# The router's comparisons behind the decays of level 2: one step moved in a hand-ordered recurrent-mixer kernel

## The chip, the cores and the metric

The kernel runs on one core of a Trainium2 chip. The metric is the time of one execution on the device, in microseconds (us). TensorE (PE), VectorE (DVE), ScalarE (ACT) and GpSimd (POOL) each work through their own queue in order, and wait for one another through semaphores; SyncE (SP) issues the transfers.

## The reference

The input is x, of 2 sequences with 2048 tokens of 256 channels, all in float32. After a layer norm, two branches read it, and the result is x + s * silu(f).

```
xn  = layernorm(x)
# s: the time mixing
dx  = previous token of xn - xn
mix = tanh((xn + dx * x_miu) @ x_A)            # six groups of 32
xd  = xn + dx * (lambdas + mix @ x_B)          # r, w, k, v, a, g
r, v, k, w, a, g = projections of the six xd   # k is normalised to length 1
S   = S * decay + (S a) b^T + v k^T ; y = S r  # per token, 4 heads of 64 x 64
s   = (groupnorm(y) + bonus(r, k, v)) * g @ oW.T
# f: eight experts, two per token
scores = softmax(xn @ gate_w.T + gate_b) ; top 2 -> which experts, and the sum of their scores
f   = sum over the chosen e of gate * (relu(xn @ wi.T + bi + lora_e(xn)) @ wo.T + bo)
```

The top 2 are found by rank: expert e's rank is the number of experts with a larger logit, plus those with an equal logit and a smaller number.

## The kernel before

The tokens are taken in 16 blocks of 256 rows (128 tokens of each of the two sequences). The recurrence of a block is not stepped token by token. In chunks of 64 tokens, the kernel builds the matrix of products between "queries" (AR, which holds a and r) and "keys" (BK, which holds b and k) by levels of run length 1, 2, 4, 8, 16 and 32, inverts it level by level beside that, and then carries the state ST over the chunks.

A block passes through six generators: `norm` (layer norm, transposes), `front` (logits, router, the mix), `mixes` (xd and the projections), `levels` (products and inverse), `chunks` (state, output) and `experts`. Time is counted in turns of 12 units. In one turn the level steps of block n-1 run beside `front` and `mixes` of block n, `chunks` of block n-2 and a share of `experts`. Each generator yields the time at which its next step is due, and the queue at the end of the kernel always runs the step with the smallest time. That fixes the order in which instructions are written, and each engine executes its own in that order. The due times are the numbers in the table `AT`, lines 96 to 107.

The names that the text uses:

- The router, in `front`. L357 (POOL) takes all differences of the logits into eq. The step "gt" follows: L359 (DVE) turns them into gt (greater), L360 (DVE) into eq (equal), L361 (POOL) masks eq and L362 (POOL) adds it to gt. The step "rank" sums gt (L365, DVE) and makes the one-hot oh (L368, DVE, twice).
- The decays, in `decay_on(h)`. After the products of level h are taken, AR is scaled (L587, DVE), BK is scaled (L590, POOL), and the product of the decays over the doubled runs is formed (bp, L592, POOL). For level 2 both are due at 1.94. The products of level 4 (lev, L552, PE) read AR and BK; the inverse step x (L637, PE) follows, is taken into X (L641, DVE), and lev is taken into D (L565, DVE), which m1p (L630, PE) reads.
- Around them: ST (L859, DVE, four per chunk, from the products uv, L846 and L854); miu (L409, PE), which is turned into xd by L415 (DVE, two per group) and L417 (POOL, one per group); the output product op (L909, PE) and the gate after it (L913, DVE); bonb (L746 and L747, POOL); the experts' lop (L951, PE), hs (L955 on DVE, L958 on ACT), hT (L959, POOL), fop (L974, PE) and gate (L976, DVE).

Most products of TensorE go to one ring of four PSUM buffers (`psf`, L63): a product takes the buffer of the fourth one before it, and waits for whoever empties that.

The masks' construction at the start (`constants`) has a step that is due at the time of "gt" too, plus 0.02.

Of the kernel before, what the change touches and what calls it, by code (L numbers as in the profile page):

```python
# [34 lines left out]
def timemix_gated_by_lora_experts(ctx: ExitStack, tc: tile.TileContext, a: dict, out: bass.AP):  # L35
# [50 lines left out]
    def load_x(i):  # L86
# [8 lines left out]

    AT = {
        "stats": 5.73, "root_x": 10.18, "inv_x": 10.27, "xn": 10.83, "xTp": 11.66, "dx": 11.66, "xm": 11.84,
        "lgp": -0.16, "mixp": 0.51, "top": 0.56, "gt": 1.93, "rank": 2.69, "ex": 3.27, "vsum": 4.02, "rp": 4.72,
        "wkp": 5.28, "vp": 6.47, "kp": 7.83, "ssp": 8.61, "dec": 9.04, "ggp": 9.37, "root_k": 9.8, "kn": 10.55,
        "av": 11.71, "rk": 12.04, "bop": 12.53, "eye": -0.33, "query1": 0.39, "key1": 0.54, "query2": 1.94,  # L100
        "key2": 1.94, "query4": 3.29, "key4": 3.49, "query8": 5.43, "key8": 5.46, "query16": 7.8, "key16": 7.86,
# [975 lines left out]
```

## Time and profile before

| | us |
|---|---|
| median of 3 runs | 1079.38 |
| lowest and highest | 1077.13 and 1079.39 |
| profiled execution, its own time | 1079.38 |
| span of its instructions | 1077.6 |
| TensorE busy | 1032.4 |
| VectorE busy | 684.7 |
| GpSimd busy | 666.9 |
| ScalarE busy | 574.8 |

The mean granted clock of TensorE is 0.988 of full speed. A line of the groups or of the timeline names line, engine, operation, and output<-inputs; a timeline line begins with start and length in us, counted from the span's start, and ends in brackets with the idle time of the engine before it and what ended it. The chain of waits is followed back from the last instruction, at each step to what released it. Moments such as 314.85 are on the scale of that span.

### The profile page before, as it was taken

The numbers are of one execution on the slowest core, as the hardware profiler recorded it, in microseconds if no ns is written. First come the engines' busy times: TensorE is split into PE (matmuls) and PEld (weight loads), VectorE is DVE, ScalarE is ACT, GpSimd is POOL, SyncE is SP. The second block draws the span as 40 slices with busy tenths as digits, with TensorE's granted clock in tenths as the row PEclk, the third lists the DMA queues.
The fourth block names the chain that finished last, engine by engine and source line by source line (L and its number), as shares of the span: only waits on it lengthen the run. The fifth ranks groups of instructions, "written<-read, shape, count | busy, mean of one in ns | idle before, by whom it ended". The sixth has DMA issues, their size and how long they took to land.

```text
span 1077.6 us, 51168 instructions
## 1 busy us (share of the span) xinstructions
PE 1032.4 (96%) x23136; PEld 809.9 (75%) x23136; DVE 684.7 (64%) x1613; ACT 574.8 (53%) x1372; POOL 666.9 (62%) x853
## 2 busy tenths in 40 slices
PE   6989999999999998999999999999999999999997
PEld 4667877877778776787777877777777778787775
DVE  5364666767676664756757586665767666666645
ACT  2534647374664736546464655546464554736362
POOL 6473766767485764838657584756757385675541
PEclk9989999999999999999999999999999999999998
DMA  7100000000000000000000000000000000000000
GB/s 217 43 2 2 3 3 4 23 3 23 3 3 23 3 23 2 17 9 4 23 3 23 3 23 3 3 23 4 23 3 13 3 4 13 3 13 3 14 3 21
DMA packets 16153, 17.05 MB, mean 16 GB/s; under 512 B 3328, under 2 KB 15552, under 8 KB 15936
## 3 DMA queue, kind: packets, MB, share of 16 engines
q1 hardware_dynamic: 15776, 13.65, 4.9%
q8 instruction: 182, 2.98, 1.1%
q14 instruction: 35, 0.29, 0.1%
q10 hardware_dynamic: 160, 0.13, 0.0%
HBM read 9.53 MB, written 4.19 MB: 13 GB/s over the span
## 4 chain that ended last, share of the span: by engine, by line
PE 84%; DVE 5%; ACT 3%; issue 1%; POOL 1%; DVEq 0%; POOLq 0%; ACTq 0%
PE fop L974 10%; PE lop L951 10%; PE basep L946 9%; PE lev L552 8%; PE m1p L630 4%; PE m1p L624 3%; PE miu L409 3%; PE rp L426 3%; PE vp L464 3%; PE kp L473 3%; PE x L637 3%; PE op L909 2%; PE mixp L337 2%; PE uv L846 2%; PE sa L816 2%; PE uv L854 1%
## 5 line engine op out<-in xcount | busy, mean ns | idle before, releaser
L959 POOL TENSOR_TENSOR hT<-hs 128x256 f32<-128x256 f32 x128 | 94.3, 737 | 185.8 <-ACT hs L958 185.5
L958 ACT ACTIVATE hs<-hs 128x512 f32<-128x512 f32 x128 | 80.4, 629 | 121.7 <-DVE hs L955 108.3
L951 PE MATMUL lop<-lat,w_lBT 128*128 128x512 f32 x256 | 136.4, 615 | 5.5 <-ACT lat L938 5.2
L955 DVE TENSOR_TENSOR hs<-lop,base 128x512 f32<-128x512 f32 x128 | 87.4, 683 | 83.5 <-PE lop L951 62.8
L946 PE MATMUL basep<-xT,w_wiT 128*128 128x256 f32 x512 | 137.2, 391 | 0.3
L417 POOL TENSOR_TENSOR xd<-xd,xT 128x512 f32<-128x512 f32 x96 | 119.5, 1274 | 13.0 <-DVE xd L415 12.9
L974 PE MATMUL fop<-w_woT,hT 128*128 128x256 f32 x512 | 125.8, 390 | 0.8 <-POOL hT L959 0.8
L946 PEld LDWEIGHTS basep<-xT,w_wiT 128*128 128x128 f32 x512 | 92.1, 191 | 39.4 <-issue 21.7
L565 DVE COPY_PREDICATED D<-mask,lev 128x512 f32<-128x512 uint8 x160 | 106.3, 716 | 16.1 <-PE lev L552 15.9
L552 PE MATMUL lev<-AR,BK 64*64 64x64 f32 x6144 | 110.3, 220 | 3.0 <-POOL BK L590 1.9
L552 PEld LDWEIGHTS lev<-AR,BK 64*64 64x64 f32 x6144 | 99.8, 134 | 16.1 <-issue 8.9
L974 PEld LDWEIGHTS fop<-w_woT,hT 128*128 128x128 f32 x512 | 94.7, 192 | 18.2 <-issue 3.5
L590 POOL TENSOR_TENSOR BK<-BK,bp 128x512 f32<-128x512 f32 x80 | 91.4, 1143 | 15.3 <-PE lev L552 15.3
L415 DVE SCALAR_TENSOR_TENSOR xd<-miu,cvec,dx 128x256 f32<-128x256 f32 x192 | 78.1, 477 | 30.5 <-PE miu L409 30.2
L948 ACT ACTIVATE base<-basep,biT 128x256 f32<-128x256 f32 x128 | 61.0, 476 | 13.2 <-PE basep L946 12.9
L630 PEld LDWEIGHTS m1p<-X,D 64*64 64x64 f32 x2560 | 47.2, 137 | 23.8 <-issue 15.6
L863 ACT COPY Y<-uv 64x128 f32<-64x128 f32 x128 | 33.3, 260 | 52.8 <-DVE ST L859 24.9
L587 DVE TENSOR_TENSOR AR<-AR,bp 128x512 f32<-128x512 f32 x80 | 58.5, 731 | 0.0
L630 PE MATMUL m1p<-X,D 64*64 64x32 f32 x2560 | 54.9, 224 | 3.6 <-DVE D L565 3.5
L641 DVE COPY_PREDICATED X<-maskT,x 128x256 f32<-128x256 uint8 x64 | 32.6, 509 | 38.5 <-PE x L637 38.5
L951 PEld LDWEIGHTS lop<-lat,w_lBT 128*128 128x128 f32 x256 | 43.3, 189 | 15.0 <-ACT lat L938 7.6
L485 POOL TENSOR_TENSOR ksq<-ksq 128x256 f32<-128x256 f32 x16 | 11.6, 727 | 64.7 <-ACT ksq L484 64.7
(218 smaller groups left out, 2369.8 us busy)
## 6 DMA issues: line engine op xcount, KB each, us to landing
x<-in_x SPq DMA_DIRECT2D x32, 128.0 KB, 2.8
out<-x SPq DMA_DIRECT2D x30, 128.0 KB, 2.4
w_wiT<-in_wiT SPq DMA_DIRECT2D x1, 1024.0 KB, 9.3
w_woT<-in_woT SPq DMA_DIRECT2D x1, 1024.0 KB, 7.9
w_lBT<-in_lBT SPq DMA_DIRECT2D x1, 512.0 KB, 6.3
w_rWT<-in_rWT SPq DMA_DIRECT2D x1, 256.0 KB, 5.0
w_vWT<-in_vWT SPq DMA_DIRECT2D x1, 256.0 KB, 8.6
w_kWT<-in_kWT SPq DMA_DIRECT2D x1, 256.0 KB, 3.2
```

Of the source, the lines that this page charges most:

```text
L415: nc.vector.scalar_tensor_tensor(xd[:, c, :], p[:, c, :], cv("lam", c, g), dx[:, c, :], ALU.add, ALU.mult)
L417: nc.gpsimd.tensor_add(xd, xd, xT)
L552: matmul(levp[par][half(b), (k * 2 + pair) * 2 + key], BK[rows, key, c0 : c0 + L], query_runs(AR[rows, c0 : c0 + L, :], h), start=True, st ...
L565: nc.vector.copy_predicated(query_runs(D[:, par, :, 0:L, :], h), mask_of(mask, li, 2 * h, 4 * NK), levp[par])
L590: nc.gpsimd.tensor_mul(ka, ka, decay(1, h).unsqueeze(1).broadcast_to([P, 2, np_, h]))
L630: matmul(m1[half(b ^ k), m], D[half(b), e % 2, (k * 2 + e // 2) * 2, 0:L, 0], runs(X[half(b), m, :], h, 0), start=True, stop=True)
L946: matmul(basep, wiT[:, c, fc], xT[:, c, :], start=(c == 0), stop=(c == 1))
L951: matmul(lop, lBT[:, 0, fc], lat, start=True, stop=True)
L955: nc.vector.tensor_tensor(hs, lop, bs.unsqueeze(1).broadcast_to([P, 2, SUP]), ALU.add)
L958: nc.scalar.activation(hs, hs, AF.Relu)
L959: nc.gpsimd.tensor_add(hT[:, f, :], hs[:, 0, :], hs[:, 1, :])
L974: matmul(fop, hT[:, f, k * P : (k + 1) * P], woT[:, f, :], start=(f == 0), stop=(f == DFF // P - 1))
```

## The change

One number of the table of due times changes. The step "gt" was due at 1.93, just ahead of the decays of level 2 (1.94); it is now due at 2.05, just behind them.

```diff
-        "lgp": -0.16, "mixp": 0.51, "top": 0.56, "gt": 1.93, "rank": 2.69, "ex": 3.27, "vsum": 4.02, "rp": 4.72,
+        "lgp": -0.16, "mixp": 0.51, "top": 0.56, "gt": 2.05, "rank": 2.69, "ex": 3.27, "vsum": 4.02, "rp": 4.72,
```

In the order of the engines' instructions this does the following, in each of the 15 turns that have both steps, and nothing else:

```
VectorE before:  L359 gt, L360 eq, L587 AR
VectorE after:   L587 AR, L359 gt, L360 eq
GpSimd before:   L361 eq, L362 gt, L590 BK, L592 bp
GpSimd after:    L590 BK, L592 bp, L361 eq, L362 gt
```

The orders of TensorE, ScalarE and SyncE are the same in both kernels.

## The prediction

> **What bounds the kernel now.** I read the page first, then the chain of waits in order of time, then the timelines of VectorE and GpSimd around the moved step, and last the busy time of TensorE by stretches. Two lines of the page's first part and its chain by engine:
>
> ```profile
> span 1077.6 us, 51168 instructions
> PE 1032.4 (96%) x23136; PEld 809.9 (75%) x23136; DVE 684.7 (64%) x1613; ACT 574.8 (53%) x1372; POOL 666.9 (62%) x853
> ...
> PE 84%; DVE 5%; ACT 3%; issue 1%; POOL 1%; DVEq 0%; POOLq 0%; ACTq 0%
> ```
>
> TensorE is busy 96% of the span and carries 84% of the chain. No instruction is added or dropped by this change, so it can only act where TensorE waits for VectorE or GpSimd. I call turn n the one in which block n's router runs beside the level steps of block n-1; there are 15, about 62 us apart. The moved step lies on the chain in two of them. In turn 1 the chain in order of time (start, length, what) reads:
>
> ```profile
> 67.81 0.14 DVE gt L359
> ...
> 67.97 0.24 DVE eq L360
> ...
> 68.28 0.84 POOL eq L361
> ...
> 69.19 0.45 POOL gt L362
> 69.65 1.26 POOL BK L590
> ...
> 70.95 1.38 PE lev L552 x64
> ```
>
> Here TensorE stood idle for 1.92 us until the key decay (BK, L590) that queued behind the comparisons. In the other turns the level-4 products start 1.5 to 4.6 us after that decay has ended, so making it earlier is worth nothing there. Turn 5 shows the other side, VectorE's lines first and GpSimd's after them (start, length):
>
> ```profile
> 313.48 0.91 DVE L359 TENSOR_SCALAR gt<-eq 128x128 f32<-128x128 f32 x1
> 314.42 0.23 DVE L360 TENSOR_SCALAR eq<-eq 128x128 f32<-128x128 f32 x1
> 314.56 1.23 DVE L587 TENSOR_TENSOR AR<-AR,bp 128x512 f32<-128x512 f32 x1
> 315.72 0.84 DVE L859 SCALAR_TENSOR_TENSOR ST<-ST,bp,uv 128x64 f32<-128x64 f32 x4
> 316.73 1.27 DVE L415 SCALAR_TENSOR_TENSOR xd<-miu,cvec,dx 128x256 f32<-128x256 f32 x3 [0.17 <-PE miu L409]
> ...
> 313.03 1.27 POOL L747 TENSOR_TENSOR bonb<-bonb,beta 128x512 f32<-128x512 f32 x1
> 314.42 0.82 POOL L959 TENSOR_TENSOR hT<-hs 128x256 f32<-128x256 f32 x1
> 315.19 0.91 POOL L361 TENSOR_TENSOR eq<-eq,lower 128x128 f32<-128x128 f32 x1
> ```
>
> The comparison takes 0.22 where GpSimd is idle (turn 1) and 0.91 here, ending 0.09 after bonb. The query decay AR takes 0.68 alone and 1.23 here, ending 0.54 after hT. The product eq (L361) takes 0.45 alone and 0.83 to 0.91 beside an AR that began first. So the two engines take turns over these three kinds, and the one that comes second waits for the end of the other's whole instruction. And TensorE does wait for what follows on VectorE:
>
> ```profile
> L909 PE MATMUL op<-w_oWT,yg x120: 379/379/483, 192.7 to 1051.1; 128*128 128x256 f32 x120
> ...
>   DVE xd L415: 8.1, 11
> ```
>
> The output product op is held by the first xd in 11 turns, since it takes the PSUM buffer that this xd empties: in turns 4 to 7 and 9 to 12 it starts 0.05 after that xd. A late xd is a late TensorE.
>
> **The change part by part.** It moves one step of four instructions in each of 15 turns and no DMA: gt and eq on VectorE go behind one AR (L587); eq and gt (L361, L362) on GpSimd go behind one BK (L590) and one bp (L592). The orders of TensorE, ScalarE and SP stay as they are, and so does the mask step that shares the time of "gt". The cost is the same work in another order, so I redo the order with the rows' durations: AR 0.68, or 0.55 after a GpSimd instruction that held it; gt 0.22, or 0.08 after one; eq 0.23 likewise; BK 1.29; bp 0.40; L361 and L362 0.45 each with 0.08 between.
>
> Turn 1: GpSimd is idle from 63.99 on (4.29 us before L361) and the level-2 products end at 64.95, so BK runs about 65.0 to 66.3. AR runs 67.72 to 68.40. The level-4 products need both, TensorE free (69.03), and a second buffer, which xd empties at 69.94. They start at about 70.0 rather than 70.95. Their inverse step then ends near 71.5. But X (L641) stands behind rank and oh on VectorE, which end at 72.6, where it now starts at 73.19. So 0.95 at the products shrinks to **-0.6** at m1p (L630).
>
> The clock belongs to the same place. The stretches (length, TensorE busy, ..., granted clock third from the end):
>
> ```profile
> 51.26:54.67 3.41, 2.12 (x11) 1.40 (x10) 1.02 (x3) 2.88 (x7) 2.23 (x4) 1.00 0.01 2
> 68.32:71.73 3.41, 1.49 (x64) 1.07 (x62) 3.12 (x9) 0.89 (x3) 3.33 (x5) 1.00 0.00 0
> 71.74:81.97 10.23, 8.68 (x142) 6.89 (x132) 7.33 (x17) 0.86 (x2) 10.11 (x13) 0.50 0.01 3
> ```
>
> After 3.41 us with 1.49 busy (44%) the clock is 0.50 for 10.23 us; after 2.12 (62%) it stays. The groups in that stretch take 1.38, 0.85, 0.86, 0.91, 2.01 and 3.46, which are 1.09, 0.44, 0.61, 0.49, 1.07 and 1.92 in later turns: 3.85 lost. With the change the idle stretch moves to 71.5 to 74.0, so I expect the drop one stretch of 3.41 later and two such stretches long in place of three: **-1.3** (bounds 0 and -3.85).
>
> Turns 5, 6, 10 and 11 lose. Turn 5: AR comes at 313.48, waits for bonb (314.30), ends at 314.85. hT came at 314.42, and is held until AR is nearly done; it ends at 315.43. gt gets in behind it (315.51). BK is next on GpSimd and already waiting, so eq, which must wait for gt, is held for all of BK and ends at 316.84. ST starts at 316.76 instead of 315.72, xd at 317.52 instead of 316.73, and op 0.79 later. Turn 6 goes the same way (bonb to 375.75, AR 376.30, hT 376.88, BK to 378.20, eq 378.29): xd 378.96 instead of 378.12, 0.84. Turn 11 (bonb to 694.22, AR 694.77, hT 695.35, BK to 696.67, eq 696.76): xd 697.44 instead of 696.27, 1.17; there gt, eq, AR, ST and xd are the chain. Turn 10: eq is held by hT alone (631.33 to 632.06), 0.45. Sum **+3.25**. Before, the pair stood in front of BK. The trace never shows BK against gt or eq; I take it from its nearest rows, bonb and hT, adds of the same engine. If it did not hold eq, only the 0.45 of turn 10 is left; if bp (0.40) got in ahead of eq too, it is 1.2 more.
>
> Knock-on, turn 6: rank moves to 381.32 and oh (L368) to 381.63, past the GpSimd boundary at 381.06 which it now meets; both oh then wait for an xd add of 1.27 each, to 383.8 instead of 381.17. D (L565) ends about 1.9 later, and fop, which has 0.45 to spare, loses about **+1.1** beyond the 0.84. In the other turns oh waits for the same add as before.
>
> Clock, turn 11: TensorE already idles 0.93 before op, and 1.17 more makes 2.1 us in one stretch. The trace's rows say that this drops the clock (1.92 idle did in turn 1). The Trainium skill ("TensorE: Matmul & The Clock Gate", section "Why this matters for your kernels") says that idle gaps have to stay below about 3 us for the clock to hold; by that this turn would keep it. I go by the row: one stretch of 3.41 at half clock, at 3.85/8.68 per busy us, **+1.5**. By the page the sum is 1.5 lower.
>
> Turns without cost, with their cover: 2, 4, 13, 14 and 15 have VectorE waiting 0.17 to 1.63 ahead of ST for the uv products, and by the same arithmetic eq ends up to 1.6 us after AR did; that wait takes most of it, ST comes at most 0.6 late, and xd there waits for miu long enough to hide the rest. Without that cover each would cost its 0.4 to 1.6. In 3 and 12 GpSimd is free, or nearly, as the three run. In 7, 8 and 9 gt or eq arrives only 0.03 to 0.04 ahead of an hT; I take it as arriving first. If it loses, 0.78, 0.51 and 0.51 come back as late xd. The new wait, rank for L362: the six GpSimd instructions still end where bp ended, 0.05 to 3 us ahead of rank, so nothing. Behind rank stand oh, hs, gate and X.
>
> Sum: -0.6 - 1.3 + 3.25 + 1.1 + 1.5 = **+3.95**. The profiled execution took 1079.38, of which 1077.6 is span; that is also the median of the runs shown. So 1083.3.
>
> **The rivals.** (a) The gain in turn 1 decides, faster. If the level-4 products and what follows keep TensorE above about 60% of each 3.41 us there, the half-clock stretch goes: -0.6 - 3.85 = -4.45. With the traps of turns 5, 6, 10 and 11 at half of 3.25 and no knock-on or second drop, 1079.38 - 4.45 + 1.6 = 1076.5. For: where the stretches' borders lie is not tied to the program by anything I see. Against: the 2.5 us idle before m1p is longer than the 1.92 that did it. (b) The two sides cancel: the traps cost 3.25, the clock in turn 1 gives 1.3 to 2.6 and there is nothing else: 1079.4 to 1080.7, no difference that can be told. (c) The three close arrivals are lost too: 0.78 + 0.51 + 0.51, and turn 7's oh, now 0.17 ahead of a boundary, goes as turn 6's did (1.1): 3.95 + 2.9, 1086.2; a further drop of the clock on one of these stalls makes it 1087.7. (d) The change does nothing: excluded for the order, since the two queues do differ.
>
> **How the numbers follow.** Forecast 0.50 (1081.6 to 1086), (a) 0.18 (1075 to 1077.2), (b) 0.20 (1077.2 to 1081.5), (c) 0.12 (1086 to 1091). A measurement of this kernel tells about 0.2%, 2.16 us, from no change. Slower: 0.50 + 0.12 = 0.62; same 0.20; faster 0.18. The range leaves out the lower part of (a) and the upper part of (c), about 0.2 together: 1077.0 to 1088.5. The likeliest case's own range is 1081.6 to 1086.
>
> **What would show it.** Right: in turns 5, 6 and 11 eq (L360) at 1.0 us or more, ending 0.1 after BK; ST and xd about 1.1 and 0.8 late against miu; TensorE idle before op up from 8.1 us by about 3; in turn 1 no idle time for BK and X near 72.6 on that scale. Wrong, if L360 stays at 0.23 in those turns, if op starts as soon after miu as before, or if the half-clock stretch in turn 1 is gone.

## The result and the profile after

The changed kernel took 1083.09 us (median of 20 runs, 1075.44 to 1088.31), the kernel before, measured beside it, 1078.48 (20 runs): a ratio of 1.0038, 95% interval 1.0024 to 1.0051. A second measurement of the changed kernel gave 1081.07 against 1079.47, 1.0014 (0.9999 to 1.0028). Weighted by the width of their intervals the two make 1.0027, or 2.9 us. The direction is the forecast one; the second interval alone just reaches no change.

The page of the changed kernel, first part and chain by engine:

```profile
span 1084.7 us, 51169 instructions
PE 1037.1 (96%) x23136; PEld 812.5 (75%) x23136; DVE 681.8 (63%) x1613; ACT 575.8 (53%) x1372; POOL 666.0 (61%) x853
...
PE 83%; DVE 6%; ACT 3%; issue 1%; POOL 1%; DVEq 0%; ACTq 0%; POOLq 0%
```

The span is 7.1 us longer than in the profile of before (its own time is 1086.51). That is more than the change does: TensorE's busy time grew by 4.7 us with the same 23136 products, because the granted clock was 0.983 instead of 0.988, and turn 6 alone is 5.3 us longer (72.02 against 66.69), with 13.65 us at half clock where before had 3.41. In the second profiled execution of the changed kernel, turn 6 takes 68.53; an execution of the order of before takes 67.71. So the turns have to be read one by one, each against the start of its level-2 products.

The line of the output product, whose wait was 8.1 us in 11 turns:

```profile
L909 PE MATMUL op<-w_oWT,yg x120: 379/379/483, 192.1 to 1058.2; 128*128 128x256 f32 x120
...
  DVE xd L415: 13.8, 14
```

Turn 5, the timeline of VectorE and then that of GpSimd (start, length):

```profile
312.83 1.39 DVE L587 TENSOR_TENSOR AR<-AR,bp 128x512 f32<-128x512 f32 x1
314.14 0.75 DVE L359 TENSOR_SCALAR gt<-eq 128x128 f32<-128x128 f32 x1
314.92 1.22 DVE L360 TENSOR_SCALAR eq<-eq 128x128 f32<-128x128 f32 x1
316.06 0.84 DVE L859 SCALAR_TENSOR_TENSOR ST<-ST,bp,uv 128x64 f32<-128x64 f32 x4
316.83 1.26 DVE L415 SCALAR_TENSOR_TENSOR xd<-miu,cvec,dx 128x256 f32<-128x256 f32 x3
...
312.40 1.27 POOL L747 TENSOR_TENSOR bonb<-bonb,beta 128x512 f32<-128x512 f32 x1
313.78 1.03 POOL L959 TENSOR_TENSOR hT<-hs 128x256 f32<-128x256 f32 x1
314.77 1.29 POOL L590 TENSOR_TENSOR BK<-BK,bp 128x512 f32<-128x512 f32 x1
316.38 0.45 POOL L361 TENSOR_TENSOR eq<-eq,lower 128x128 f32<-128x128 f32 x1
```

This is the forecast sequence link by link: bonb holds AR, hT comes next and is stretched by AR, gt follows hT, BK follows gt, and eq ends at 316.14, 0.08 after BK (316.06). ST and xd follow at once, with no wait for miu left. In turn 11 the same makes TensorE wait (the bracket is its idle time before the line):

```profile
703.98 1.99 PE L909 MATMUL op<-w_oWT,yg 128*128 128x256 f32 x8 [2.04 <-DVE xd L415]
```

Turn 1, TensorE and then the key decay on GpSimd:

```profile
69.02 0.33 PE L552 MATMUL lev<-AR,BK 64*64 64x64 f32 x2
70.04 1.10 PE L552 MATMUL lev<-AR,BK 64*64 64x64 f32 x59 [0.70 <-DVE xd L415]
...
74.00 0.32 PE L630 MATMUL m1p<-X,D 64*64 64x32 f32 x8 [2.36 <-DVE D L565]
...
65.21 1.30 POOL L590 TENSOR_TENSOR BK<-BK,bp 128x512 f32<-128x512 f32 x1 [1.16 <-PE lev L552]
```

BK now ends at 66.5, the products wait for an xd instead (70.04, forecast 70.0), and m1p starts at 74.00 where it started at 74.61.

Beside each other, from the timelines, in us after the start of the level-2 products:

| turn | op before | op after | m1p before | m1p after |
|---|---|---|---|---|
| 1 | | | 10.82 | 10.15 |
| 5 | 7.54 | 8.27 | 15.42 | 16.15 |
| 6 | 7.49 | 8.27 | 15.36 | 16.14 |
| 7 | 8.41 | 8.41 | 15.42 | 15.81 |
| 8, 9 | same | same | 15.73 | 15.41 |
| 10 | 7.60 | 7.94 | 15.85 | 15.81 |
| 11 | 9.27 | 10.37 | 16.27 | 17.38 |
| 12 | same | same | 15.53 | 14.98 |
| 13 | same | same | 15.63 | 14.96 |

Turns 2, 3, 4, 14 and 15 do not move. Most of turn 1's 0.67 is a matter of the clock and not of the order, as all_but_turn1 shows below. The gains in 8, 9, 12 and 13 were not forecast; they are taken up in the last group of experiments.

### The profile page after: what moved, and what is told of

It is laid out like the page before. It is cut to its first block, busy times and chain, and to the rows that moved or that the text cites. A ratio compares the mean times of both kernels' runs of the same rounds, so it can differ in the third digit from the quotient of the medians.

```text
span 1084.7 us, 51169 instructions
## 1 busy us (share of the span) xinstructions
PE 1037.1 (96%) x23136; PEld 812.5 (75%) x23136; DVE 681.8 (63%) x1613; ACT 575.8 (53%) x1372; POOL 666.0 (61%) x853
## 3 DMA queue, kind: packets, MB, share of 16 engines
q1 hardware_dynamic: 15776, 13.65, 5.0%
## 4 chain that ended last, share of the span: by engine, by line
PE 83%; DVE 6%; ACT 3%; issue 1%; POOL 1%; DVEq 0%; ACTq 0%; POOLq 0%
PE fop L974 11%; PE lop L951 9%; PE basep L946 9%; PE lev L552 8%; PE m1p L630 4%; PE m1p L624 3%; PE rp L426 3%; PE miu L409 3%; PE vp L464 3%; PE kp L473 3%; PE x L637 2%; PE op L909 2%; PE mixp L337 2%; PE sa L816 2%; PE uv L846 2%; PE zp L477 1%
## 5 line engine op out<-in xcount | busy, mean ns | idle before, releaser
L951 PE MATMUL lop<-lat,w_lBT 128*128 128x512 f32 x256 | 138.6, 623 | 4.8 <-ACT lat L938 4.7
L417 POOL TENSOR_TENSOR xd<-xd,xT 128x512 f32<-128x512 f32 x96 | 119.8, 1277 | 19.6 <-DVE xd L415 19.4
L587 DVE TENSOR_TENSOR AR<-AR,bp 128x512 f32<-128x512 f32 x80 | 61.8, 773 | 0.0
```

The costliest lines, as they stand in the source:

```text
L417: nc.gpsimd.tensor_add(xd, xd, xT)
L951: matmul(lop, lBT[:, 0, fc], lat, start=True, stop=True)
```

## The experiments

The theory, T: eq is held by BK, and so ST, xd and op come late in turns 5, 6, 10 and 11, while turn 1 gains. Rivals: R, that AR held by bonb is enough to delay what follows it; C, that the time goes into a lower granted clock, and not into the order. For C the times are also compared at one clock: over all runs of this study a run is 0.50 us shorter for each 0.001 more of mean clock, among runs of one kernel, and I use that slope to bring each kernel's mean to a clock of 0.988. Before then stands at 1078.8 ± 0.2 (135 runs; ± is twice the standard error), and at 1078.8 in each of the three groups of measurements. This takes out what a change does through the clock, too, so it only answers C. The clock falls in turn 6 and near the end in all versions, for varying lengths of time.

**The change again, and in two parts.** The changed kernel once more; the new order in turn 1 alone; the new order in all turns but 1.

```diff
         # turn1_only, in the kernel before
-        yield base + AT["gt"]
+        yield base + (2.05 if i == 1 else AT["gt"])
         # all_but_turn1, in the kernel before
-        yield base + AT["gt"]
+        yield base + (AT["gt"] if i == 1 else 2.05)
```

> The changed kernel once more, for the granted clock of every run beside those of the kernel before on the same chip. Theory T (turn-taking): eq (L360) stands behind BK (L590) in turns 5, 6 and 11, xd comes late, and op (L909) waits 13.8 us for xd in place of 8.1; about 4 us slower, and about as much slower at equal clock. Rival C (clock): in one execution the turns add up to only 1.5 us of later work, and the rest is TensorE at half clock; then the mean clock of these runs is about 0.985 against 0.989 before, and at equal clock the two kernels lie less than 2 us apart.

> The step gt is moved in turn 1 alone. T: the level-4 products of turn 1 start 2 us earlier and m1p 0.65 us earlier, eq is 0.23 us in turns 5, 6 and 11 as before, op waits 8.1 us for xd; about 0.7 us faster than before, which a few runs can't tell from nothing. C, if the lower clock comes from the stalls of turns 5 to 11: the clock is that of the kernel before. If the lower clock comes from turn 1 instead, it is as low as after the change and the time about 2 us above before.

> The step gt is moved in turns 2 to 15 and stays in turn 1. T: op waits about 13.8 us for xd; turn 1 has TensorE idle for 1.9 us as before; slower than the changed kernel by 0.7 us, so about 5 us above before. C: the clock as low as after the change, about 0.985.

Measured: after_again 1.0014 (0.9999 to 1.0028), turn1_only 1078.06 us, 0.9986 (0.9972 to 1.0), all_but_turn1 1081.6 us, 1.0015 (1.0001 to 1.0029). The waits of op, all_but_turn1 and then turn1_only:

```profile
  DVE xd L415: 13.8, 14
```

```profile
  DVE xd L415: 8.1, 11
```

The loss is in the other turns: all_but_turn1 has op as late as the changed kernel, and turn 1 with its idle 1.92 us before the products of level 4. It was expected to be 0.7 us slower than the changed kernel, and is not: at one clock it is at 1080.2 ± 0.9, and after_again at 1080.5 ± 0.9. Turn1_only leaves op where it was. Its gain of 1.5 us just reaches no change, and at one clock there is none (1078.9 ± 0.7): its clock was higher (0.9891 on average, against 0.9863 for before beside it). For all_but_turn1 the clock was low, as C had it (0.9847), but 1.4 us of its loss remain at one clock. C falls with after_again: its clock (0.9869) is not below before's, and at one clock it is still 1.7 us slower.

Why turn 1 gains so little stands in turn 1 of all_but_turn1, which has the order of before. The kernel before first, then all_but_turn1:

```profile
72.08 1.04 PE L637 MATMUL x<-M,Z 64*64 64x32 f32 x32
73.19 0.72 DVE L641 COPY_PREDICATED X<-maskT,x 128x256 f32<-128x256 uint8 x1 [0.60 <-PE x L637]
```

```profile
71.96 0.62 PE L637 MATMUL x<-M,Z 64*64 64x32 f32 x32
74.06 1.38 PE L630 MATMUL m1p<-X,D 64*64 64x32 f32 x32 [1.48 <-DVE D L565]
```

In before the clock was at half from 71.73 on: x took 1.04 us, and X had to wait for it. In all_but_turn1 the clock fell at 72.59, x took 0.62, X came right behind oh, and m1p stands 10.24 after the level-2 products, only 0.09 later than in the changed kernel. So the order alone is worth about 0.1 us at m1p of turn 1. The length of the turn goes with the stretches at half clock, in all 14 profiles: 61.9 to 62.8 us with three of 3.41 (after_keys_halved, with the new order, among them: 61.95), 61.3 to 61.5 with two, 59.7 to 59.9 with one. And in the four profiles with one, after_again among them, the clock falls again in turn 2 for two stretches, and turn 2 takes 63.6 us, where it takes 60.4 to 60.5 in the profiles without a drop there.

**Is it BK?** The key decay of level 2 in two instructions of half the size, so that what is caught behind one is held half as long; once in the changed kernel and, as a control, in the kernel before.

```diff
-            nc.gpsimd.tensor_mul(ka, ka, decay(1, h).unsqueeze(1).broadcast_to([P, 2, np_, h]))
+            if h == 2:
+                for j in range(2):
+                    kj = runs(BK[:, j, :], h, 0)
+                    nc.gpsimd.tensor_mul(kj, kj, decay(1, h))
+            else: ...
```

> The changed kernel with the key decay of level 2 (BK, L590) written as two instructions of 128x256 in place of one of 128x512. T: eq is held by one half only, about 0.65 us rather than 1.2, so that xd and op are late by about 0.1, 0.15 and 0.5 us in turns 5, 6 and 11 in place of 0.73, 0.78 and 1.10; op waits about 10 us for xd; 1.5 to 2 us faster than the changed kernel at equal clock, and about as fast as before. A rival R, that AR waiting for bonb (the query decay first on VectorE) is what makes xd late and not eq behind BK: then halving changes nothing, op waits 13.8 us and the time is that of the changed kernel.

> The kernel before with the key decay of level 2 in two instructions: the control for the halving by itself. T: no comparison stands behind BK here, so halving gives nothing but 0.15 us more on GpSimd; op waits 8.1 us, and in turn 1 the level-4 products come 0.15 us later; time as before within 0.5 us.

Measured: after_keys_halved 1078.5 us, 0.9993 (0.998 to 1.0007), and 1078.2 ± 0.7 at one clock, 2.3 to 3.3 below the changed kernel. Its turn 5, VectorE and GpSimd:

```profile
315.62 0.76 DVE L359 TENSOR_SCALAR gt<-eq 128x128 f32<-128x128 f32 x1
316.41 0.66 DVE L360 TENSOR_SCALAR eq<-eq 128x128 f32<-128x128 f32 x1
317.00 0.84 DVE L864 SCALAR_TENSOR_TENSOR ST<-ST,bp,uv 128x64 f32<-128x64 f32 x4
...
316.25 1.44 POOL L593 TENSOR_TENSOR BK<-BK,bp 128x256 f32<-128x256 f32 x2
```

Eq takes 0.66 instead of 1.22: it gets in between the halves. Op is late by 0.17, 0.21 and 0.55 in turns 5, 6 and 11, where it was 0.73, 0.78 and 1.10, and its wait for xd in all is 10.2. In these turns the dose follows the size of BK, which is the step of the forecast that no row of before could show. In turn 10, where eq (0.78) stands behind hT and not BK, op is 0.54 late.

The control missed its expectation: before_keys_halved took 1082.62 us, 1.0032 (1.002 to 1.0045). Halving costs the kernel before about as much as it saves the changed one. What could be found of the cause is below.

**Which engine's move does it?** The new order on VectorE alone (the due time of AR put ahead of gt), and on GpSimd alone:

```diff
         # query_first_only
-        ... "query2": 1.94,
+        ... "query2": 1.92,
         # keys_first_only, between L360 and L361 of the kernel before
+        yield base + 2.05
```

> The kernel before with the query decay AR of level 2 ahead of the comparisons on VectorE, and the old order on GpSimd (eq, gt, BK, bp). T: behind hT GpSimd then has eq (L361), which needs L360 first, so BK can't get in ahead of it; L360 stays at 0.23 us in turns 4, 5, 6 and 11, xd and op come as before the change (op waits about 8.1 us for xd), and BK and the level-4 products of turn 1 come 0.2 to 0.5 us later than before. Time within 1 us of before. Rival R (AR being held by bonb is what costs): xd late by 0.7 to 1.1 us in turns 5, 6 and 11 as in the changed kernel, and about 1.5 to 4 us slower than before.

> The kernel before with the key decay BK and bp of level 2 ahead of eq and gt on GpSimd, and the old order on VectorE (gt, eq, AR). T: turn 1 gains its 0.67 us; in turn 11 eq is held by hT and then AR, not eq, stands behind BK: AR about 1.3 us there, op 1.1 us late; in turns 5 and 6 the same wherever hT gets in ahead of eq, else nothing. op waits between 9 and 13 us for xd; 0 to 2 us slower than before. R: as fast as before or 0.7 faster, since the order on VectorE is the old one and op waits 8.1 us.

Measured: query_first_only 1079.1 us, 1.0004 (0.9987 to 1.002). Its turn 5, VectorE:

```profile
316.76 1.40 DVE L587 TENSOR_TENSOR AR<-AR,bp 128x512 f32<-128x512 f32 x1
318.08 0.76 DVE L359 TENSOR_SCALAR gt<-eq 128x128 f32<-128x128 f32 x1
318.87 0.23 DVE L360 TENSOR_SCALAR eq<-eq 128x128 f32<-128x128 f32 x1
319.01 0.85 DVE L859 SCALAR_TENSOR_TENSOR ST<-ST,bp,uv 128x64 f32<-128x64 f32 x4
320.02 1.27 DVE L415 SCALAR_TENSOR_TENSOR xd<-miu,cvec,dx 128x256 f32<-128x256 f32 x3 [0.16 <-PE miu L409]
```

AR is held for 1.40 and gt for 0.76 as in the changed kernel, but with L361 and not BK next on GpSimd, eq takes its 0.23. Xd still waits 0.16 for miu, and op starts 7.54 after the products, as before; in turn 6 the same, and in turn 11 it is 0.11 late instead of 1.10. R falls for these turns. Op's wait for xd is 9.0 all the same, not the 8.1 expected: in turn 10 eq, now behind AR, is held by hT (0.78), and op is 0.46 late. In turn 1 nothing is gained: m1p comes at 11.53, against 10.82, 11.28 and 10.24 in three executions of the order of before.

keys_first_only: 1076.45 us, 0.9985 (0.9967 to 1.0002), not the 0 to 2 us slower that was expected. Now gt and eq are past before BK comes, and in turns 5 and 6 op is as before; m1p of turn 1 keeps the gain (10.15). Only in turn 11 is AR itself caught by BK, shown here by a second execution of that kernel, VectorE and GpSimd:

```profile
693.17 1.79 DVE L588 TENSOR_TENSOR AR<-AR,bp 128x512 f32<-128x512 f32 x1
...
693.11 1.30 POOL L591 TENSOR_TENSOR BK<-BK,bp 128x512 f32<-128x512 f32 x1
```

AR begins 0.06 after BK and ends 0.55 after it; op is 1.1 late, and its wait for xd is 10.4. So the turns differ: in 5 and 6 the cost needs both moves, the keys moved up and VectorE's small instructions moved behind AR, into their way; in 11 the keys alone do it, and in 10 the queries alone.

**Does eq get caught because it waits for gt?** In the changed kernel eq overwrites what gt reads, and so waits for gt's end. Here it is written to a tile of its own:

```diff
+        dif, eq = eq, sb1.tile([P, NK, E, E], F32, tag="eqo", name=f"eqo{i}")
-        nc.vector.tensor_scalar(eq, eq, 0.0, None, ALU.is_equal)
+        nc.vector.tensor_scalar(eq, dif, 0.0, None, ALU.is_equal)
```

> The changed kernel with the equal-comparison (L360 there) written to a tile of its own, so that it no longer waits for the greater-comparison before it. T: the two go through in one turn between hT and BK, eq about 0.16 to 0.25 us instead of 1.2 in turns 4, 5, 6 and 11; xd and op as before the change, op waits 8 to 9 us for xd; turn 1 keeps its gain; about 2.5 us faster than the changed kernel and about 1 us faster than before. If GpSimd still gets in between the two (the pair oh does it in some turns and not in others), nothing changes in those turns.

Measured: 1082.56 us (6 runs), 1.0041 (1.0025 to 1.0056). Turn 5, VectorE and GpSimd:

```profile
314.98 0.75 DVE L359 TENSOR_SCALAR gt<-eq 128x128 f32<-128x128 f32 x1
315.65 1.33 DVE L361 TENSOR_SCALAR eqo<-eq 128x128 f32<-128x128 f32 x1
...
315.61 1.29 POOL L591 TENSOR_TENSOR BK<-BK,bp 128x512 f32<-128x512 f32 x1
```

There is no gap between gt and eq any more, and BK still gets in between, in turns 4, 5, 6 and 11: the wait is not what lets it in there, and the 2.5 us that this version should have gained did not come. In turns 7, 10 and 15, where eq stood behind hT or bonb and not BK, the wait did matter: eq takes 0.21 where the changed kernel had 0.64, 0.71 and 1.33. In turn 15 it starts at 945.00, ahead of a bonb at 945.08 that comes 0.08 after another instruction of GpSimd. What decides between this turn and turn 5 is not shown.

**How far does a measured ratio spread by itself, and why did the control cost 3 us?** The order of before from another due time (1.932, no queue differs), the control again, keys_first_only again, and a version that the runs so far point to: the keys first on GpSimd, except in turns 10 and 11.

```diff
         # keys_first_not_10_11, between L360 and L361 of the kernel before
+        if i not in (10, 11):
+            yield base + 2.05
```

> The order of before, from another due time (1.932 for 1.93): no queue differs. It measures what the comparison itself spreads. All theories expect a ratio of 1.000; since two measurements of the changed kernel gave 1.0038 and 1.0014, I expect a miss of up to 0.0015 from 1. op waits 8.1 us for xd, 11 times. If its ratio is off by more than 0.002, the two measurements of the changed kernel do not differ by more than chance, and neither does before_keys_halved.

> The control of the halved key decay once more. If the 3.4 us that it cost the first time belong to the kernel, the ratio is 1.002 to 1.0045 again. If they were chance in where the clock's windows fell, it is 0.999 to 1.002. The traced turns of the first time differ by 0.1 to 0.2 us each in seven turns and 0.9 in turn 12, so I expect about +1 us, 1.001.

> The decay of the keys alone ahead of the comparisons' second half on GpSimd; VectorE keeps the order of before. Measured 0.9985 [0.9967, 1.0002] with 3 rounds. If the gain of turn 1 (0.67 us, and 0 to 1.6 of clock) and of turn 13 (0.64) less the 1.1 of turn 11 are what it does, it is -0.2 to -1.8 us: 0.9983 to 0.9998. m1p of turn 1 at 10.15 after the start of the products of level 2, op's wait for xd 10.4 us.

> As keys_first_only, but turns 10 and 11 keep the order of before, so that nothing of the traps is left. Theory: op's wait for xd back to about 8.1 us, 11 times; turn 1 and 13 keep their -0.67 and -0.64; time -1.3 to -2.9 us against before, 0.9973 to 0.9988, and 1.1 us below keys_first_only. Rival (the gain of turn 1 is eaten by the stretches at half clock elsewhere): same as before, 1.000.

Measured: before_again 0.9999 (0.9988 to 1.001), so a measured ratio spreads by about 0.1%. The control 1.0021 (1.0009 to 1.0033): its loss is real, and larger than the 1.001 I expected. Turn 6 shows it. First before_again, then the second profile of the control, both on VectorE:

```profile
381.17 0.27 DVE L365 TENSOR_REDUCE rank<-gt 128x16 f32<-128x128 f32 x1
381.47 0.38 DVE L368 TENSOR_SCALAR oh<-rank 128x16 f32<-128x16 f32 x2
```

```profile
381.77 0.28 DVE L365 TENSOR_REDUCE rank<-gt 128x16 f32<-128x128 f32 x1
382.08 1.67 DVE L368 TENSOR_SCALAR oh<-rank 128x16 f32<-128x16 f32 x2
```

The two small oh take 0.30 and 0.16 in the one, 0.44 and 1.31 in the other. The second oh gets in directly behind the first, or it waits for one more xd add (L417, 1.25 each) of GpSimd. The halved decay takes 1.44 instead of 1.30, and the row of xd adds that follows begins 0.13 later against rank. With that, the second oh is long in 12 of 15 turns, where it was in 9 (before) and 6 (before_again); m1p is late by 0.76, 0.71 and 0.73 in turns 6, 7 and 13 against before_again. The first profile of the control shows less: the second oh is long in 9 turns, the same ones as in before, and in turns 8, 9, 10, 12 and 13 m1p is 0.14 to 0.15 late against before, in turn 7 0.19. So the race accounts for a part of the control's loss that differs between executions; that it is the whole is not shown.

That two executions of one and the same order differ (turns 8, 9 and 13) says how close this race is. In the changed kernel the second oh takes 0.16 in all 15 turns of both profiled executions: there the race is won, and the gains of turns 8, 9, 12 and 13 in the table are that. It goes with the order on GpSimd: over all profiles the second oh is long in 5 to 12 turns where eq and gt stand ahead of BK, and in at most one where BK is first.

keys_first_only_again: 1077.93 us, 0.9993 (0.998 to 1.0006), op's wait 10.4 as expected. keys_first_not_10_11: 1075.21 us (7 runs), 0.996 (0.9938 to 0.9982), faster than both kernels. Its span and op's wait:

```profile
span 1072.0 us, 51169 instructions
...
  DVE xd L417: 8.2, 11
```

Nothing of the traps is left, the gain of turn 1 is kept, and the second oh is short in 14 of 15 turns. The ratio is better than what was expected (0.9973 to 0.9988, of which the interval takes in the part up to 0.9982); part of it is clock (0.9894 on average): at one clock it is 1076.5 ± 1.3, 2.3 below before.

## Why the prediction was right, step by step

The forecast was 1083.3, +3.95; measured were +4.1 and +1.5. The path holds: eq behind BK, then ST, xd and op. Of the sum's terms the traps hold, turn 1 was counted twice over, the knock-on failed, the second drop of the clock came in some executions only, and turn 7 was not in it.

- **Traps in turns 5, 6, 10 and 11**, forecast 0.79, 0.84, 0.45 and 1.17, together 3.25: op came 0.73, 0.78, 0.34 and 1.10 late, 2.95. Right, in cause and size. The bound that had no row (does BK hold eq?) came out as the value taken: bp did not get in as well. That it is BK was shown by halving it. In turn 10 the lateness is gone again at m1p, where the second oh is short (0.16, before 1.32).
- **Op's wait**, forecast up by about 3 from 8.1: up by 5.7. That view adds two waits, of the products themselves (1.9 before, 4.5 after) and of the load of their weights (6.2 and 9.2). The forecast took the sum of both for idle time of TensorE; each alone grew by about 3.
- **Turn 1**, −0.6 in the order and −1.3 in the clock, −1.9: m1p came 0.67 earlier, and the products of level 4 when forecast. But the two terms count one thing twice. X at 73.19, from which the −0.6 was taken, was held by an x at half clock; at full clock X comes right behind oh in both orders, and the order is worth 0.1. The drop did come one stretch later and two stretches long, as forecast, and the turn took 61.32 us instead of 61.98: −0.66 in all. In the other profile of the changed kernel it was one stretch, 59.75, and turn 2 then lost 3.2 us to the clock, which was in no term.
- **Knock-on in turn 6**, +1.1: did not occur. Rank and oh came when I said (381.35 and 381.66, forecast 381.32 and 381.63), but the second oh did not wait for a second add; the pair took 0.90. m1p of turn 6 is 0.78 late, which is op's 0.78 and nothing more. The failed assumption was that each of two successive small instructions on VectorE waits for a whole add: the second one is a close race, and the new order wins it in all 15 turns of both profiles; why it does is not shown. That also gives back 0.3 to 0.7 in turns 8, 9, 12 and 13, when the execution of before had lost it there.
- **Turn 7**, taken as free: hT did get in ahead of eq (0.64 instead of 0.23), though xd was not late; the first oh then took 1.23 instead of 0.23, and m1p is 0.39 late. That is part of rival (c), with a third of the 1.1 that it had for turn 7's oh and nothing of its 0.78; turns 8 and 9 had no trap.
- **Clock drop in turn 11**, +1.5: it happens in some executions. With TensorE idle for 2.0 us before op, the changed kernel kept its clock in both profiles. Two others with the same idle time, all_but_turn1 and keys_first_only_again, lost it for one stretch, and turn 11 then took 65.8 and 65.7 instead of 64.1 us: 1.6, as sized. The stretches of turn 11 differ in how busy TensorE was. The changed kernel first, then keys_first_only_again (length, TensorE busy, ..., granted clock third from the end):

```profile
72.05:75.46 3.41, 1.28 (x64) 1.16 (x64) 3.41 (x8) 0.00 (x0) 3.41 (x4) 1.00 0.00 0
75.46:82.28 6.82, 6.82 (x68) 4.78 (x64) 3.07 (x10) 1.49 (x3) 6.74 (x10) 0.50 0.01 2
700.09:703.50 3.41, 1.85 (x16) 1.05 (x10) 3.38 (x9) 0.26 (x2) 3.33 (x5) 1.00 0.03 5
```

```profile
692.95:696.36 3.41, 1.57 (x13) 0.78 (x7) 3.41 (x8) 0.52 (x3) 3.13 (x5) 1.00 0.02 5
696.37:699.77 3.40, 3.20 (x8) 2.58 (x9) 2.79 (x8) 1.26 (x4) 3.18 (x3) 0.50 0.00 0
```

The same idle time leaves 54% of a stretch busy in the one and 46% in the other, depending on where the stretch's border falls. The row that I had gone by (1.92 idle dropped the clock in turn 1) let me expect a drop every time, though that stretch was 44% busy; the Trainium skill's rule ("TensorE: Matmul & The Clock Gate", section "Why this matters for your kernels", gaps below about 3 us are safe) would let one expect none, and with the same gap the clock did drop in keys_first_only_again. In this turn the share of a stretch tells the cases apart, and the forecast should have carried this term with a chance and not whole.

So the mechanism was right, and the sum came near partly by luck: the forecast's 1.1 of knock-on and 1.5 of clock mostly did not occur, turn 1 was over-sized, and in their place there are 0.39 in turn 7, gains of the oh, and a lower mean clock in the first measurement (0.9852). Read off at m1p over all turns, with a gain of 0.1 for turn 1, the order alone costs 1.0 against one profiled execution of before and 2.3 against the other, which lost fewer of the oh races; at one clock the two measurements say +2.7 and +1.7, each ± 0.9. Two profiles of each kernel are few for more than that, since the oh and the turns with half clock differ between executions. The difference between the two measurements of the changed kernel is not explained.

## What to carry to other kernels

When two engines get in each other's way, a small instruction can cost what stands ready at the head of the other queue, and not its own length (eq here 1.22 us in place of 0.23): before moving a step, list for every small instruction which one of the other engine comes next at that moment, and keep the long ones from that place. Move a step per engine and per turn where its due time allows it: here the gains belong to the order on GpSimd, and which engine's move brings the loss differs between the four turns. Before counting an earlier start as a gain of the order, look whether the instruction that held it was running at half clock: then it may belong to the clock term. A split of the long instruction is no free remedy: here it took 0.14 us more, and in the kernel before it cost about 3 us.

## What the runs showed of the hardware

- An instruction of GpSimd can get in between two back-to-back instructions of VectorE even where the second does not wait for the first (eq in its own tile in turns 4, 5, 6 and 11: 1.33 us for 0.22 of work). It is not always so: in turn 15 the same eq took 0.21.
- In a close race a small shift of GpSimd's queue (0.13 us in turn 6 of the control) goes with 1.15 us on VectorE (the second oh, 0.16 or 1.31), 0.7 of it at m1p, and the same order of instructions falls on either side of it in different executions.
- The granted clock of TensorE changes in steps of 3.41 us: between its first and its last change every stretch at one clock is a whole number of these (3.41, 6.83, 10.24, 13.65 at half clock). In turn 11, stretches with 42 and 46% busy lost it (all_but_turn1, keys_first_only_again) and those with 53 and 54% did not (keys_first_only, the changed kernel); elsewhere one of 44% did (turn 1, before), one of 62% did not, but one of 52% (turn 1, after_keys_halved, 1.79 us from 70.26 on), one of 61% (turn 2, after_again, 2.07 of the 3.41 us from 133.75 on) and one of 57% did (near 1027.8, changed kernel):

```profile
1027.77:1031.18 3.41, 1.96 (x88) 1.70 (x81) 2.99 (x6) 0.88 (x2) 1.09 (x2) 1.00 0.00 0
```

  The share of busy time is therefore not all there is to it.
- After a drop one to four stretches pass before the clock is back, in the same place of the program, in different executions; over all runs the time of a run of one kernel moves with the mean clock by 0.50 us per 0.001.
